# Building the last sixteen heads' convolution kernels during the first down stage instead of between two convolutions

## The chip, the cores and the metric

The kernel runs on one core of a Trainium2 chip. The metric is the device time of one execution in microseconds; the time of a version is the median over its runs.

## The reference

The input x has the shape (32, 64, 1024): 32 sequences in the batch, 64 heads, 1024 positions. Two stages follow one another, and x is added to the result.

```python
# stage 1: a state space convolution, one kernel of length 1024 per head
dtA = A * dt[:, None]                       # A = -exp(log_A_real) + i*A_imag, 64 states a head
K = 2.0 * einsum('hn,hnl->hl', C * (exp(dtA) - 1) / A, exp(dtA[:, :, None] * arange(1024))).real
u_m = u * mask                              # positions past a sequence's length are zero
y = causal_convolution(u_m, K) + u_m * D    # by FFT in the reference
y = y * mask
# stage 2: a gated feed-forward net over y as 2048 rows (32 x 64) of 1024, weights of 4 bits
inter = silu(y @ Wg) * (y @ Wu)             # Wg, Wu: 1024 x 2752, one scale and zero point per 128 rows
out = inter @ Wd                            # Wd: 2752 x 1024, likewise
x = x + out
```

## The kernel before, in words

**Blocks and stages.** The 2048 rows of stage 2 are cut into four blocks of 512, each of 16 heads times 32 sequences. Block 0 needs the convolutions of heads 0 to 15, block 1 those of 16 to 31, block 2 of 32 to 47 and block 3 of 48 to 63. The call `conv(blk)` makes a block's input; this text calls conv(2) the third convolution and conv(3) the fourth (by its index, the fourth is number 3). An input block lies in on-chip memory as two float16 tiles of 128 x 8 x 512, a rounded part and a remainder. There are two such pairs, `c.x[0]` and `c.x[1]`: blocks 0 and 2 use the first, 1 and 3 the second.

Matrix work is a list of chains that `roll` runs through (L773). Stage 0 and 1 are the first gate and up products of blocks 0 and 1, stage 2 (`pairs`) the rest of these for both blocks at once, stage 3 the down products of block 0, stage 4 those of block 1, stage 5 the gate and up products of blocks 2 and 3, stages 6 and 7 their down products. In stages 3 and 4 nothing reads `c.x[1]`, from the last gate and up product of stage 2 until the fourth convolution writes it.

**A chain.** A down chain (`dn_pair`, L718) takes 21 groups of 128 rows and half a group: for each it issues four matmuls (L732, L733), and then the sum in PSUM has to be multiplied by the ratio of two scales before the next group can be added. This rescale runs on VectorE (L637, one instruction over two banks) or on ScalarE (L640, two of one bank), whichever the planner expects to be done first (`rescale_two`, L635). Three chains are in work at a time in stages 3 and 4, so that TensorE has matmuls of two chains while the third is being rescaled. A down step below means the four matmuls of one group.

**A convolution head.** `conv_head` (L531) multiplies a Toeplitz matrix of the head's kernel with the head's input: 24 matmuls (L548) of 32 to 256 columns. The matrix tile, 128 x 2 x 1024 float16 or 512 KB, is read from `kpad` in DRAM by a load on the SP queue (`toeplitz`, L525), whose source rows overlap. Three buffers hold such tiles, and the load of a tile is placed three heads ahead, so it waits until the head three before it has been multiplied. Every two heads the product is masked (L560, VectorE), rounded (L563, ScalarE) and its remainder taken (L565, mostly POOL). Every four heads an input `u` is loaded (L503) and split (L507, L510).

**A convolution kernel.** It is made for 8 heads at a time: decays (`decays`: L175 on POOL, an Exp over 16 heads on ScalarE at L179), phases (`tables`: L192 to L204 on VectorE, Sin and Square at L207 and L209 on ScalarE), factors (L218 to L223, VectorE), then `make_kernel` (L421): one matmul for the skip term D (L425), eight small ones (L427), two copies out of PSUM (L430, L431) and two writes to `kpad` on the SP queue (L433).

**Who sets the order.** Side work is written as generators, listed by stage in `sides` (L1033). For each step of a chain `roll` adds a side's rate to its credit and takes a step of it for each whole credit. Sides whose third entry is None take a step only while the planner's clocks of VectorE and ScalarE are not far ahead of TensorE's (`room`, L327); the others take it in any case, and those marked True are finished before the stage is left. `c.forced` turns off the planner's pauses. The framework then orders each engine's instructions by priority and its own estimate of readiness.

In stages 3 and 4 the sides are the unpacking of the down weights, `fourth()` and `convs()`. `fourth()` (L996) makes the kernels of heads 48 to 63. It waits until all down weights are unpacked, closes the unpacking buffers and opens a pool `kg2` in their place; the decays lie in `c.x[1][0]`, the phases in `c.x[1][1]`, factors and kernels in `kg2`. `convs()` (L1017) runs the third convolution, then whatever is left of `fourth()` at one go with `c.forced` set, then the fourth. Its rate is 1.9 steps (eight make a head) for one step of a chain (`RATES`, L33).

Of the kernel before, what the change touches and what calls it, by code (L numbers as in the profile page):

```python
# [29 lines left out]
KSCALE = 64.0  # L30
PLACES = {("a", "pair"): 1, ("a", "single"): 2, ("b", "pair"): 3}
MAGIC = 12582912.0
RATES = {"first": (0.5, 4.6), "fill": (1.0, 0.8), "third": 0.5, "convs": 1.9}  # L33
HOP, MM, LANDING = 220.0, 215.7, 6000.0
LAG, HEAD_START, APART = 2, 2, 5
DVE_ROOM, ACT_ROOM = 1200.0, 1500.0
# [211 lines left out]
def every(gen):  # L248
    for _ in gen:
        pass  # L250
# [585 lines left out]
def tile_ssm_ffn(ctx, tc, io):  # L836
    nc = tc.nc
    c = Core(ctx, tc, io)
# [119 lines left out]
    def third():  # L958
        tiles = [c.cv.tile([128, 2, L], F16, name="t0", bufs=3) for _ in range(3)]
        small = [c.cv.tile([128, 8, 4, B], F16, name=k) for k in ("uh", "ul", "uh", "ul")]  # L960
        take = c.scratch(tiles[:2])
        c.prm = take([128, 5, H], F32)
        nc.sync.dma_start(c.prm, io["prm"])
        for _ in range(4):
            yield
        coefficients = head_coefficients(nc, nc.vector, co, take, c.prm, c.cst[:, 66:67], 32, 32)
        while True:
            with c.after("dve"), c.after("act"):
                if next(coefficients, "end") == "end":
                    break  # L970
            c.dve(1000)
            yield
        yield from c.decays(c.scratch(tiles[2:]), (32, 40))
        c.small = ScratchPool(c.scratch(small))
        c.taps(c.small, 32)
        for h0 in (32, 40):
            yield from c.tables(ScratchPool(c.scratch(tiles[:2])), h0, 8)
            yield from c.factors(c.small, h0, 8, c.xds[h0])

    third_it = third()  # L980
# [13 lines left out]
        return make  # L994

    def fourth():  # L996
        c.forced = True
        every(third_it)
        c.forced = False
        while not c.ready.issuperset(("dn", k, part) for k in range(4) for part in range(3)):  # L1000
            yield
        c.up_stack.close()
        with tc.tile_pool(name="kg2", bufs=1, side="right") as kg2:
            space = c.x[1]
            yield from c.decays(c.scratch(space[:1]), (48, 56))
            c.taps(kg2, 48)
            for h0 in (48, 56):
                yield from c.tables(ScratchPool(c.scratch(space[1:])), h0, 8)
                yield from c.factors(kg2, h0, 8, c.xds[h0])
                for _ in range(3):  # L1010
                    yield
                c.make_kernel(kg2, h0, 8, "a")
                yield

    fourth_it = fourth()

    def convs():  # L1017
        yield from c.conv(2)
        c.forced = True
        c.need(*(("dn", k, part) for k in range(4) for part in range(3)))  # L1020
        every(fourth_it)
        c.forced = False
        yield from c.conv(3)

    def residuals():
        take = c.scratch(c.x[0])
        c.res = [c.residual(take, n0, 3) for n0 in (0, 2, 4, 6)]
        c.last_o = c.scratch(c.x[1])
        yield

    convs_it = convs()
    second_it = second()
    sides = {  # L1033
        0: [(unpack_it, RATES["first"][0], None), (group_it, 1.0, None), (second_it, RATES["first"][1], True)],
        1: [(unpack_it, RATES["fill"][0], None), (third_it, RATES["fill"][1], None)],
        2: [(third_it, RATES["third"], None), (unpack_it, RATES["fill"][0], None)],
        3: [(unpack_it, RATES["fill"][0], None), (fourth_it, RATES["fill"][1], None), (convs_it, RATES["convs"], False)],
        4: [(fourth_it, RATES["fill"][1], None), (convs_it, RATES["convs"], True)],
        6: [(residuals(), 1.0, True)],
# [80 lines left out]
```

## Time and profile before

| | |
|---|---|
| median of 3 runs | 1079.41 us (1079.26 to 1080.23) |
| the profiled execution | 1076.19 us |
| its span, first to last instruction | 1074.4 us |
| TensorE busy | 1025.0 us, 95% |
| VectorE, ScalarE, POOL busy | 804.7, 773.7, 243.9 us |
| granted clock of TensorE | 0.997 |
| stages 3 and 4 with the third and fourth convolution | 400.1 us (first matmul of head 32) to 577.7 us (last of head 63) |
| heads 32 to 47, heads 48 to 63 | 400.1 to 485.4 us, 509.0 to 577.7 us |

The page gives busy times of one profiled execution by engine; the windows give the same for any stretch of it. PE stands for TensorE's matmuls, PEld for its weight loads, DVE for VectorE, ACT for ScalarE. A matmul is shown with its whole way through the array, so two neighbours overlap: a product of 512 columns is shown as 0.38 us, while the next one starts 0.216 us later. In a timeline the square brackets give an engine's idle time before an instruction, and after the arrow who ended it.

### The profile page before, as it was taken

The numbers are of one execution on the slowest core, as the hardware profiler recorded it, in microseconds if no ns is written. First come the engines' busy times: TensorE is split into PE (matmuls) and PEld (weight loads), VectorE is DVE, ScalarE is ACT, GpSimd is POOL, SyncE is SP. The second block draws the span as 40 slices with busy tenths as digits, with TensorE's granted clock in tenths as the row PEclk, the third lists the DMA queues.
The fourth block names the chain that finished last, engine by engine and source line by source line (L and its number), as shares of the span: only waits on it lengthen the run. The fifth ranks groups of instructions, "written<-read, shape, count | busy, mean of one in ns | idle before, by whom it ended". The sixth has DMA issues, their size and how long they took to land.

```text
span 1074.4 us, 15424 instructions
## 1 busy us (share of the span) xinstructions
PE 1025.0 (95%) x5854; PEld 512.6 (48%) x5854; DVE 804.7 (75%) x938; ACT 773.7 (72%) x1031; POOL 243.9 (23%) x272
## 2 busy tenths in 40 slices
PE   3989999999899999997999999999999999999996
PEld 3867444444344445663665444444444444444442
DVE  8964888888977786678456777777778777777775
ACT  5767778787677787778577777666666667778774
POOL 0334123232332333230112112222221111102002
PEclk9999999999999999999999999999999999999998
DMA  6976321111111424455752011000000002325002
GB/s 196 332 243 211 100 69 40 40 59 40 49 50 58 139 90 156 152 180 190 238 167 99 30 38 42 20 20 20 18 13 20 20 20 79 118 72 166 37 1 79
DMA packets 52099, 99.76 MB, mean 93 GB/s; under 512 B 9524, under 2 KB 11444, under 8 KB 52024
## 3 DMA queue, kind: packets, MB, share of 16 engines
q1 hardware_dynamic: 38888, 70.09, 20.1%
q0 software_dynamic: 5280, 17.31, 4.3%
q10 hardware_dynamic: 7856, 11.37, 3.6%
q8 instruction: 46, 0.75, 0.3%
q14 instruction: 29, 0.24, 0.1%
HBM read 78.99 MB, written 19.76 MB: 92 GB/s over the span
## 4 chain that ended last, share of the span: by engine, by line
PE 81%; DVE 7%; ACT 5%; DMA 3%; issue 2%; POOL 1%; DVEq 0%; SPq 0%; ACTq 0%; POOLq 0%
PE chq L687 23%; PE chq L688 22%; PE chq L732 12%; PE chq L733 12%; PE cq L548 6%; PE chq L664 2%; PE chq L665 2%; DMA t<-kpad 2%; ACT chq L640 1%; DVE chq L618 1%; DVE v L700 1%; ACT chq L620 1%; DMA ihl<-kpad 1%; ACT sg L695 1%; POOL spill L310 0%
## 5 line engine op out<-in xcount | busy, mean ns | idle before, releaser
L687 PE MATMUL chq<-xh,w 128*128 128x512 f16 x1216 | 459.4, 379 | 7.2 <-DVE chq L618 2.1
L688 PE MATMUL chq<-xl,w 128*128 128x512 f16 x1216 | 457.6, 379 | 0.0
L618 DVE TENSOR_SCALAR chq<-chq,gur 128x1024 f32<-128x1024 f32 x261 | 333.3, 1290 | 93.4 <-PE chq L688 91.8
L620 ACT ACTIVATE chq<-chq,gur 128x1024 f32<-128x1024 f32 x285 | 304.2, 1085 | 86.9 <-PE chq L688 84.4
L640 ACT ACTIVATE chq<-chq,dnr 128x512 f32<-128x512 f32 x358 | 232.8, 661 | 68.6 <-PE chq L733 62.8
L732 PE MATMUL chq<-ihl,wd 128*128 128x512 f16 x672 | 253.0, 379 | 8.9 <-ACT chq L640 5.2
L733 PE MATMUL chq<-ihl,wd 128*128 128x512 f16 x672 | 252.9, 379 | 0.0
L637 DVE TENSOR_TENSOR chq<-chq,dnr 128x1024 f32<-128x1024 f32 x141 | 173.1, 1230 | 81.0 <-PE chq L733 80.2
L688 PEld LDWEIGHTS <-w 128*128 128x128 fp8e4 x1216 | 118.6, 98 | 154.6 <-issue 18.5
L687 PEld LDWEIGHTS <-w 128*128 128x128 fp8e4 x1216 | 118.7, 98 | 146.7 <-issue 1.1
L310 POOL TENSOR_TENSOR ihl<-v,ihl 128x512 f16<-128x512 f32 x42 | 48.3, 1150 | 364.0 <-ACT ihl L629 364.0
L733 PEld LDWEIGHTS <-wd 128*128 128x128 fp8e4 x672 | 65.4, 97 | 81.0 <-issue 18.2
L548 PEld LDWEIGHTS <-t 128*128 128x128 f16 x1152 | 81.3, 98 | 38.7 <-DMA t<-kpad 5.8
L732 PEld LDWEIGHTS <-wd 128*128 128x128 fp8e4 x672 | 65.4, 98 | 67.2 <-issue 0.8
L548 PE MATMUL cq<-uh,t 128*128 128x256 f16 (+3 forms) x720 | 91.1, 226 | 4.1 <-DMA t<-kpad 4.0
L565 POOL TENSOR_TENSOR xl<-y,xh 128x512 f16<-128x512 f32 x28 | 36.4, 1301 | 161.0 <-ACT xh L563 161.0
L548 PE MATMUL cq<-ul,t 128*128 128x256 f16 (+3 forms) x360 | 71.6, 225 | 0.0
L629 ACT CAST ihl<-v 128x512 f16<-128x512 f32 x42 | 25.9, 617 | 58.7 <-DVE v L700 55.3
L700 DVE SCALAR_TENSOR_TENSOR v<-chq,gul,sg 128x1024 f32<-128x1024 f32 x38 | 48.6, 1280 | 17.2 <-PE chq L688 11.3
L310 POOL TENSOR_TENSOR spill<-v,spill 128x512 f16<-128x512 f32 x42 | 48.8, 1161 | 14.2 <-ACT spill L629 13.9
L640 ACT ACTIVATE chq<-chq,gur 128x512 f32<-128x512 f32 x66 | 43.2, 661 | 11.0 <-PE chq L665 9.8
L590 POOL TENSOR_TENSOR w<-w,z 128x256 int32<-128x256 int32 x42 | 31.6, 772 | 81.2 <-DVE w L584 76.9
(249 smaller groups left out, 812.5 us busy)
## 6 DMA issues: line engine op xcount, KB each, us to landing
t<-kpad SPq DMA_DIRECT2D x48, 512.0 KB, 4.3
spill<-spill POOLq DMA_DIRECT2D x42, 256.0 KB, 2.7
ihl<-spill ACTq DMA_DIRECT2D x42, 256.0 KB, 2.7
z<-zc SPq DMA_DIRECT2D x29, 256.0 KB, 3.7
u<-xF SPq DMA_DIRECT2D x12, 512.0 KB, 3.9
xr<-xT SPq DMA_DIRECT2D x12, 512.0 KB, 4.5
out<-xr POOLq DMA_DIRECT2D x24, 256.0 KB, 2.9
w<-qgu SPq DMA_DIRECT2D x21, 256.0 KB, 4.8
```

The lines of the kernel that those rows point to most:

```text
L310: self.nc.gpsimd.tensor_tensor(out, a, b, op)
L548: nc.tensor.matmul(q[:, d:, h % 2, :], t0[:, lw, 128 * d:128 * d + 128], uu[:, 0:8 - d, h % 4, :], start=(d == 0 and k == 0 and h % 2 == 0 ...
L565: split.tensor_tensor(xl[:, :, ts], yv, xh[:, :, ts], ALU.subtract)
L618: self.mark("dve", self.nc.vector.tensor_scalar(q, q, col, None, ALU.mult))
L620: self.mark("act", self.nc.scalar.activation(q, q, AF.Copy, scale=col))
L637: self.mark("dve", self.nc.vector.tensor_tensor(q, q, cols.to_broadcast([128, 2, 512]), ALU.mult))
L640: self.mark("act", self.nc.scalar.activation(q[:, k], q[:, k], AF.Copy, scale=cols[:, k]))
L687: nc.tensor.matmul(q[:, b], lw, xh[:, g, :], start=(g == 0), stop=False, skip_group_check=True)
L688: nc.tensor.matmul(q[:, b], lw, xl[:, g, :], start=False, stop=(g == GH - 1), skip_group_check=True)
L700: nc.vector.scalar_tensor_tensor(v, q, last, self.sg.pop(ct - 21), ALU.mult, ALU.mult)
L732: nc.tensor.matmul(q[:, j], lw, self.ihl[:, g, 0], start=(g == 0), stop=False, skip_group_check=True)
L733: nc.tensor.matmul(q[:, j], lw, self.ihl[:, g, 1], start=False, stop=False, skip_group_check=True)
```

## The change

`fourth()` no longer waits for the unpacked weights nor for the unpacking buffers: it starts with stage 3. All that it needs lies in the idle `c.x[1]`: decays in the first half of `c.x[1][0]`, the taps in a quarter of it, phases in seven eighths of `c.x[1][1]`, factors and kernels in what is left of both. The pause before `make_kernel` is now the planner's lead of VectorE over TensorE plus 220 ns, in place of three steps. `convs()` no longer runs `fourth()` at one go: after the third convolution it yields, step by step, until the kernel of heads 56 to 63 is known, and drives `fourth()` itself only when it is forced. The rate of `convs()` falls from 1.9 to 1.52 steps.

```diff
-RATES = {"first": (0.5, 4.6), "fill": (1.0, 0.8), "third": 0.5, "convs": 1.9}
+RATES = {"first": (0.5, 4.6), "fill": (1.0, 0.8), "third": 0.5, "convs": 1.52}
...
     def fourth():
-        c.forced = True
-        every(third_it)
-        c.forced = False
-        while not c.ready.issuperset(("dn", k, part) for k in range(4) for part in range(3)):
+        first, second = c.x[1]
+        yield from c.decays(c.scratch([first[:, :4]]), (48, 56))
+        c.taps(ScratchPool(c.scratch([first[:, 4:6]])), 48)
+        for h0 in (48, 56):
+            small = ScratchPool(c.scratch([first[:, 6:8], second[:, 7:8]]))
+            yield from c.tables(ScratchPool(c.scratch([second[:, :7]])), h0, 8)
+            yield from c.factors(small, h0, 8, c.xds[h0])
+            yield from c.pause(c.td - c.tp + HOP)
+            c.make_kernel(small, h0, 8, "a")
             yield
-        c.up_stack.close()
-        with tc.tile_pool(name="kg2", bufs=1, side="right") as kg2:
-            space = c.x[1]
-            yield from c.decays(c.scratch(space[:1]), (48, 56))
-            c.taps(kg2, 48)
-            for h0 in (48, 56):
-                yield from c.tables(ScratchPool(c.scratch(space[1:])), h0, 8)
-                yield from c.factors(kg2, h0, 8, c.xds[h0])
-                for _ in range(3):
-                    yield
-                c.make_kernel(kg2, h0, 8, "a")
-                yield
...
     def convs():
         yield from c.conv(2)
-        c.forced = True
-        c.need(*(("dn", k, part) for k in range(4) for part in range(3)))
-        every(fourth_it)
-        c.forced = False
+        while 56 not in c.known:
+            if c.forced:
+                next(fourth_it)
+            yield
         yield from c.conv(3)
```

## The prediction

> **What bounds the kernel now.** I read the page first, then the busy time by window, then the TensorE timeline where the windows showed a hole, then the loads of the Toeplitz tiles.
>
> The page names TensorE:
>
> ```profile
> span 1074.4 us, 15424 instructions
> PE 1025.0 (95%) x5854; PEld 512.6 (48%) x5854; DVE 804.7 (75%) x938; ACT 773.7 (72%) x1031; POOL 243.9 (23%) x272
> ```
>
> The change leaves the number of matmuls as it is, so it can gain only where PE waits. The windows (PE, PEld, DVE, ACT, POOL busy, then clock and DMA) say where:
>
> ```profile
> 425.00:475.00 50.00, 50.00 (x398) 30.46 (x397) 34.06 (x41) 36.46 (x56) 13.67 (x18) 1.00 0.47 151
> 475.00:485.00 10.00, 9.69 (x82) 5.93 (x80) 8.14 (x9) 6.67 (x11) 5.35 (x7) 1.00 0.79 261
> 485.00:517.00 32.00, 24.11 (x198) 13.49 (x197) 23.00 (x39) 22.56 (x37) 1.77 (x3) 1.00 0.65 209
> 517.00:567.00 50.00, 50.00 (x399) 30.41 (x397) 26.31 (x25) 36.32 (x56) 8.03 (x8) 1.00 0.58 183
> ```
>
> PE is never idle from 425 to 475 and from 517 to 567, and idles 7.9 us from 485 to 517. That is where `convs()` runs the whole of `fourth()` at once, between the third and the fourth convolution. The timeline shows its six long waits (start, duration, then the idle time and who ended it):
>
> ```profile
> 491.62 0.38 PE L732 MATMUL chq<-ihl,wd 128*128 128x512 f16 x1 [1.45 <-ACT chq L640]
> ...
> 494.98 0.38 PE L732 MATMUL chq<-ihl,wd 128*128 128x512 f16 x1 [1.48 <-DVE chq L637]
> ...
> 498.27 0.38 PE L732 MATMUL chq<-ihl,wd 128*128 128x512 f16 x1 [1.14 <-ACT chq L640]
> ...
> 502.89 0.38 PE L732 MATMUL chq<-ihl,wd 128*128 128x512 f16 x1 [1.85 <-ACT chq L640]
> ...
> 508.98 0.28 PE L548 MATMUL cq<-uh,t 128*128 128x256 f16 x1 [0.87 <-DMA t<-kpad]
> ...
> 511.67 0.28 PE L548 MATMUL cq<-uh,t 128*128 128x256 f16 x1 [1.00 <-DMA t<-kpad]
> ```
>
> Four times a down chain waits for its rescale, which stands behind table work on VectorE or ScalarE; twice the convolution waits for its first Toeplitz tiles. Every number rests on the load of such a tile (L525, 512 KB), issue to landing, from 425 to 475 and from 505 to 520:
>
> ```profile
> DMA to landing us min/median/max: 3.4/3.6/4.6
> ...
> DMA to landing us min/median/max: 3.7/4.9/6.0
> ```
>
> **What goes.** The six waits sum to 7.79 us. A matmul is shown as 0.38 us but the next starts 0.216 later, so each wait hides 0.16 more: 8.8. Two shorter holes (starts 0.27 and 0.15 later than that pitch, at 495.62 and 499.65) make 9.2 us. The kernel matmuls L425 and L427 stay and cost the same.
>
> **What is moved, and stays as much.** From the groups between 405 and 585: VectorE's table, factor and copy work for 16 heads (L192 to L204 9.1 us, L218 to L223 4.0, L431 0.8) is 13.9 us; ScalarE's (two table loads 2.6, L179 1.1, L207 2.0, L209 2.0, L430 0.7) is 8.4. POOL's two L175 stand where they stood in the built order. In it the work now lies among the rescales of the first down stage and of the early second one: the kernel of heads 48 to 55 comes half way through head 43, that of 56 to 63 at the end of head 47. There VectorE is 68% and ScalarE 73% busy (34.06 and 36.46 of 50). The fourth group's steps are taken only while the planner has room, so rescales go to the other engine. Low bound: nothing, as 425 to 475, where unpacking of weights is taken in the same way, loses nothing. High bound: 9.2 us, what the same 22.3 us of work costs in its present place. The nearest dense stretch is 395 to 405, where VectorE is busy 9.18 and ScalarE 9.66 of 10 us and PE idles 0.59. I take 1.5 us, that rate over some 25 us of the added work.
>
> For the table loads row and rule differ. The rows, of ScalarE's timeline:
>
> ```profile
> 484.07 1.36 ACT L640 ACTIVATE chq<-chq,dnr 128x512 f32<-128x512 f32 x2 [1.08 <-PE chq L733]
> 485.45 1.28 ACT L179 ACT_TABLE_LOAD   x1
> 486.74 1.06 ACT L179 ACTIVATE xh<-xh 128x1024 f32<-128x1024 f32 x1
> ```
>
> The load begins 0.02 us after the rescale before it, and its Exp begins as it ends. The Trainium skill (ScalarE: Activation LUTs, What ACT_TABLE_LOAD costs) adds a drain of some 1380 ns to each switch, which would speak against putting two switches among rescales: an estimate from it is 2.8 us more on ScalarE, and a forecast of -1.1 instead of -3.9 if all of it fell on the path. The trace shows no such drain, so it is not in the sum.
>
> **Queues passed.** On SP the tap load L440 now waits, ahead of two residual loads and a tile load, for the last gate/up read of x[1]; head 35's tile behind it waits for head 32 anyhow: nothing. The four kpad writes (L433) stand ahead of tile loads 46 and 51, two residual loads (L768, which wait for output DMAs to land) ahead of 46 and 47: tile 46 is issued by my count some 5 us before its head, against a load of 3.6; nothing, and one for one if it is over 1.4 us later. The first output of heads 48 and 49 must wait until x[1]'s scratch has been read; it stands 13 down steps of 0.86 us (four matmuls) after the last kernel: covered. No later Sin or Silu load is added: the built order has ten table loads in both.
>
> **What is added: a burst.** `convs` runs at 1.52 steps instead of 1.9 for each step of a chain, also while it waits for head 56. The built order shows the result. Before, the 64th head ends together with the 133rd down step, matmuls of both mixed to the end. After, at that step only head 55 and two matmuls of head 56 are done; the second down stage ends its share, the convolution must be finished (it is marked True), and 190 convolution matmuls follow without a down matmul between them, heads 56 to 63. Nothing else is left for PE in that time.
>
> One head takes 1.54 us (511.67 to the next matmul at 513.21). There are three tile buffers: the tile of head h+3 can be issued only when head h has ended. With a load L, 0.1 us to trigger and wake (an estimate; the issue at 510.70 follows head 48's last matmul, which ends at 510.68) and 1.54 us of matmuls, three heads take L + 1.64 instead of 4.62. Counted from the burst's start: head 55 ended at -1.08, so tile 58 is issued then; 56 ends at 1.40, 57 at 2.95. With L = 4.9, the median where loads followed one another: 58 starts 3.95 (1.0 late) and ends 5.5; 59 starts 6.4 (0.9 late), ends 7.95; 60 is in time, ends 9.5; 61 starts 10.5 (1.0), ends 12.05; 62 starts 12.95 (0.9), ends 14.5; 63 ends 16.05. Lost: 3.8 us. With L = 3.4, the shortest, 0.8 us; with 6.0, the longest here, 6.0 us. I take 3.8: in the burst's first half the outputs of two chains (four of 256 KB) move too, as in the stretch that gave 4.9. The Trainium skill (DMA: Bandwidth & Descriptors, Anatomy of one DMA) has a rule of 2.0 us plus bytes over 436 GB/s; for 512 KB that is an estimate of 3.2 us, a loss of 0.4 and a sum of -7.3. The rows are above it wherever loads follow one another, so they decide.
>
> After the burst both orders are alike (first gate/up of x[0], eight down matmuls between), so the 0.77 us wait at 580.01 stays.
>
> **The sum.** -9.2 + 1.5 + 3.8 = -3.9 us. The profiled run took 1076.19 us, 3.2 under the median of the runs, 1079.41; so 1072.3 for a profiled run and 1075.5 for the median.
>
> **Rivals.** *The burst is nearly free* (tiles land in 3.4 us, table work is hidden): -9.2 + 0.8 = -8.4, 1071.0. For it: the lone loads from 425 to 475. Against: 4.9 at 505 to 520.
>
> *The burst eats the gain*: L = 6.0 with outputs and a residual load beside it, 6.0, and 1 to 4 us of rescales: -2.2 to +0.8, 1077.2 to 1080.2. For it: 5.96 for one load at 505.67, and 3.7 MB of tiles in some 16 us beside 1 MB of outputs, with 209 GB/s over 485 to 517. Against: loads there come in pairs after a pause, those of the burst one by one.
>
> *Slower: the table work costs its rescales as much wherever it stands.* In the hole 22.3 us of it cost 9.2, 0.41 us for each. If three chains without slack pay the same in the first down stage, nothing is gained and the burst is added: +3.8, 1083.2. It is slower by 0.2% from 7.6 us on, 0.34 for each us. For it: rescales are in order behind the tables, and convolution matmuls that fill their waiting are thinner (1.52). Against: it is no longer forced, and 425 to 475 has 15.9 us of free VectorE.
>
> That the change does not do what it says is answered by the order: the kernel of heads 48 to 55 now stands inside the third convolution, and the fourth follows with no stretch of table work before it.
>
> **How the numbers follow.** A measurement of this kernel tells 0.2%, 2.2 us, from no change. Forecast (-2.2 to -7, so 1072.4 to 1077.2) 0.47; nearly free 0.15; eaten 0.18; slower 0.20. Faster: 0.62, same 0.18, slower 0.20. The range starts at the cheap burst, 1071.0, and ends at 1082.5, which leaves out about half of the slower case.
>
> **What would show it.** Right: no PE wait over 1 us between 485 and 550 (my count puts the burst at 556 to 573); then a stretch of some 16 us with L548 alone on PE, four waits of about 1 us for t<-kpad, convolution over near 573.8; VectorE and ScalarE near idle in it. Wrong: waits for L637 or L640 spread over 410 to 500 that sum to more than 5 us; tile loads over 6 us in the burst; or a tile load held behind an L433 or L768 on SP.

## The result and the profile after

The changed kernel takes 1081.02 us (median of 20 runs, 1078.49 to 1082.19) against 1078.69 us for the kernel before (20 runs, 1076.26 to 1083.9). The ratio is 1.0020, with a 95% interval of 1.0011 to 1.0028: slower by 2.2 us (1.2 to 3.0), where 3.9 us less had been forecast. The profiled execution took 1081.07 us. The page of the kernel after begins:

```profile
span 1079.3 us, 15440 instructions
...
PE 1028.1 (95%) x5854; PEld 513.3 (48%) x5854; DVE 813.0 (75%) x942; ACT 767.6 (71%) x1023; POOL 245.4 (23%) x272
```

The span is 4.9 us longer than before, with the same 5854 matmuls. Not all of this is the change: the execution profiled before took 1076.19 us, 2.5 less than its median, the one after lies at its median. TensorE was held up for longer, or ran at a lower clock, in some stretch. The windows of the kernel after (busy time of PE, PEld, DVE, ACT and POOL, then clock, DMA share, GB/s) say where:

```profile
425.00:475.00 50.00, 48.52 (x356) 27.91 (x355) 39.94 (x53) 37.25 (x60) 13.47 (x17) 1.00 0.41 130
475.00:485.00 10.00, 10.00 (x82) 5.74 (x81) 7.99 (x13) 8.49 (x15) 4.00 (x5) 1.00 0.76 231
485.00:517.00 32.00, 29.94 (x204) 16.27 (x203) 23.78 (x28) 19.10 (x32) 3.68 (x5) 0.95 0.74 234
517.00:567.00 50.00, 49.79 (x387) 29.96 (x386) 28.24 (x28) 38.41 (x60) 9.01 (x10) 1.00 0.58 182
567.00:585.00 18.00, 12.53 (x169) 10.72 (x168) 5.79 (x7) 3.49 (x6) 5.82 (x7) 1.00 0.59 198
```

From 485 to 517 PE idles 2.1 us in place of 7.9, so the hole has gone. But 425 to 475, which lost nothing before, now loses 1.5 us, and the clock in 485 to 517 is 0.95. The last line is new: 18 us with the convolution almost alone on PE, which idles 5.5 us of them, while VectorE and ScalarE are busy 5.8 and 3.5 us. That is the forecast burst. Its waits, from PE's timeline:

```profile
567.88 0.28 PE L548 MATMUL cq<-uh,t 128*128 128x256 f16 x1 [0.16 <-DMA t<-kpad]
572.67 0.28 PE L548 MATMUL cq<-uh,t 128*128 128x256 f16 x1 [3.10 <-DMA t<-kpad]
575.24 0.28 PE L548 MATMUL cq<-uh,t 128*128 128x256 f16 x1 [0.87 <-DMA t<-kpad]
579.04 0.28 PE L548 MATMUL cq<-uh,t 128*128 128x256 f16 x1 [0.58 <-DMA t<-kpad]
581.49 0.28 PE L548 MATMUL cq<-uh,t 128*128 128x256 f16 x1 [0.76 <-DMA t<-kpad]
```

One wait of 3.1 us stands among three of 0.6 to 0.9, near the forecast size of about 1 us. Its tile, of head 59, was issued at 566.23 and was there at 572.67: 6.4 us. By the completion signals in the trace the six loads of the burst (heads 58 to 63) took 4.2, 6.4, 7.4, 6.9, 4.6 and 4.5 us. The second to fourth of them were on the way together, and the wait for the second hid most of the lateness of the next two. Four outputs of 256 KB were issued from 564.6 to 568.8, beside those three loads, and took 4.0 to 6.3 us; the same four outputs took 2.3 to 2.8 us in the kernel before, where they started at 576.4 to 579.5 with no tile load beside them.

What else PE waited for from 400 to 600 (line that waited, who ended it, us in total, times, longest):

```profile
PE cq L548 <- DMA t<-kpad: 5.5, 5, 3.1
PE chq L732 <- DVE o L751: 2.3, 2, 2.0
PE chq L732 <- DVE wd L599: 0.8, 1, 0.8
PE chq L732 <- ACT chq L640: 0.6, 2, 0.3
```

Waits for rescales have almost gone (0.6 us). In their place stands one of 2.0 us for L751, the scaling of a finished down chain on VectorE, which frees the bank for the next chain. VectorE, POOL and PE around it:

```profile
484.03 1.38 DVE L201 SCALAR_TENSOR_TENSOR xl<-xl 128x256 f32<-128x256 f32 x1
485.33 1.64 DVE L203 SCALAR_TENSOR_TENSOR xl<-xl,cst 128x512 f32<-128x512 f32 x1
...
487.29 0.74 DVE L751 TENSOR_SCALAR o<-chq,dnl 128x512 f16<-128x512 f32 x1
```

```profile
483.60 1.53 POOL L565 TENSOR_TENSOR xl<-y,xh 128x512 f16<-128x512 f32 x1 [0.98 <-ACT xh L563]
485.09 1.33 POOL L760 TENSOR_TENSOR xr<-xr,o 128x512 f32<-128x512 f32 x1
```

```profile
488.08 0.38 PE L732 MATMUL chq<-ihl,wd 128*128 128x512 f16 x1 [2.04 <-DVE o L751]
...
491.07 0.63 PE L733 MATMUL chq<-ihl,wd 128*128 128x512 f16 x1
491.50 0.63 PE L732 MATMUL chq<-ihl,wd 128*128 128x512 f16 x1
```

L751 stands behind the second group's phases. Two of these took 1.38 and 1.64 us while POOL worked; in the hole before, with POOL idle, they took 0.41 and 0.74 us. The difference, 1.9 us, is about the whole wait. Soon after it, from 488.94 until 492.35, PE ran at half its clock: a down matmul is shown as 0.63 us and the next starts 0.43 later, in place of 0.38 and 0.216.

For the experiments TensorE's time lost is counted as well: for each pair of matmuls, the distance of their starts less the usual one for that number of columns, summed from 395 to 590. It comes to 14.0 us before and 17.8 after, in one execution each.

| stretch, us | before | after |
|---|---|---|
| 440 to 485 | 0.8 | 3.5 |
| 485 to 515 | 9.9 | 4.6 |
| 560 to 590 | 1.4 | 7.2 |

### The profile page after: what moved, and what is told of

It is laid out like the page before. It is cut to its first block, busy times and chain, and to the rows that moved or that the text cites. A ratio compares the mean times of both kernels' runs of the same rounds, so it can differ in the third digit from the quotient of the medians.

```text
span 1079.3 us, 15440 instructions
## 1 busy us (share of the span) xinstructions
PE 1028.1 (95%) x5854; PEld 513.3 (48%) x5854; DVE 813.0 (75%) x942; ACT 767.6 (71%) x1023; POOL 245.4 (23%) x272
## 4 chain that ended last, share of the span: by engine, by line
PE 77%; DVE 8%; ACT 6%; issue 5%; DMA 3%; POOL 1%; SPq 0%; DVEq 0%; POOLq 0%; ACTq 0%
PE chq L687 21%; PE chq L688 21%; PE chq L732 12%; PE chq L733 12%; PE cq L548 5%; PE chq L665 2%; PE chq L664 2%; ACT chq L640 2%; DMA t<-kpad 2%; DVE chq L618 1%; DVE v L700 1%; ACT chq L620 1%; DMA ihl<-xF 1%; POOL spill L310 1%; ACT sg L695 1%
## 5 line engine op out<-in xcount | busy, mean ns | idle before, releaser
L640 ACT ACTIVATE chq<-chq,dnr 128x512 f32<-128x512 f32 x350 | 227.5, 661 | 75.2 <-PE chq L733 68.5
L637 DVE TENSOR_TENSOR chq<-chq,dnr 128x1024 f32<-128x1024 f32 x145 | 177.1, 1230 | 75.5 <-PE chq L733 75.0
L565 POOL TENSOR_TENSOR xl<-y,xh 128x512 f16<-128x512 f32 x28 | 36.8, 1313 | 126.6 <-ACT xh L563 126.6
```

What stands on the lines that cost most here:

```text
L565: split.tensor_tensor(xl[:, :, ts], yv, xh[:, :, ts], ALU.subtract)
L637: self.mark("dve", self.nc.vector.tensor_tensor(q, q, cols.to_broadcast([128, 2, 512]), ALU.mult))
L640: self.mark("act", self.nc.scalar.activation(q[:, k], q[:, k], AF.Copy, scale=cols[:, k]))
```

## The experiments

A ratio is always to the kernel before, from runs on the same chip; one thousandth is 1.08 us. The question is which of three things gave the hole's gain back: the table work among the rescales, the late tile loads of the burst, or the new pace of the convolutions.

### The changed kernel without its tables, without its late loads, without both

The first run drops the decays, phases and factors of heads 48 to 63 and keeps the planner's bookings and the order; the second gives heads 58 to 63 an older tile in place of a load; the third does both.

```diff
-        yield from c.decays(c.scratch([first[:, :4]]), (48, 56))
+        for _ in range(4):
+            yield
+        c.act(4000)
...
-            yield from c.tables(ScratchPool(c.scratch([second[:, :7]])), h0, 8)
-            yield from c.factors(small, h0, 8, c.xds[h0])
+            c.fac[h0] = [plain.tile([128, 8, 32], F32, name=k) for k in ("e1t", "e2t")]
+            for e in c.fac[h0]:
+                nc.gpsimd.memset(e, 0.0)
...
```

```diff
-                self.t0[k] = self.toeplitz(k)
+                self.t0[k] = self.toeplitz(k) if k < 58 else self.t0[k - 3]
```

> The changed kernel without the table work of heads 48 to 63: their decays, phases and factors are left out (the factors are set to zero by POOL), so their convolution kernels hold the skip term alone and the output is not the reference's. The planner's bookings and pauses stay, so matmuls and the burst of eight heads stand as in the changed kernel. Theory A (the changed kernel pays twice: about 6.3 us in the burst, about 7 us to table work among the rescales between 440 and 495 us): that second loss goes, 2.3 - 6.5, about 4 us faster than before. Theory B (the burst is the cost, and the losses from 440 to 495 come from the thinner convolution, the change of stages and the loads queued there, with or without tables): within 1.5 us of the changed kernel, about 2 us slower than before.

> The changed kernel without the loads of the Toeplitz tiles of heads 58 to 63: each takes the tile of the head three before it, so the output is not the reference's. The matmuls stand in the same order. Theory A (in the burst PE waits for these loads): the waits of 3.1, 0.9, 0.6 and 0.8 us go, about 5.5 to 6 us faster than the changed kernel, 3 to 4 faster than before. Rival (the burst waits for the masking of its products, or for the split of its input, which the loads only hide): under 2 us faster than the changed kernel.

> Both left out: table work of heads 48 to 63 and tile loads of heads 58 to 63. If theory A's two losses are separate they add: about 2.3 - 6.5 - 6 = 10 us faster than before. If one feeds the other (the table work delays outputs and loads, which then crowd the burst), less than the sum: 6 to 8 us faster.

Measured: without tables 1076.49 us, 0.9992 (0.9984 to 1.0001); without late loads 1073.74 us, 0.9964 (0.9951 to 0.9976); without both 1071.04 us, 0.9941 (0.9929 to 0.9952). Against 1.0020 the tables cost 3.0 us, the loads 6.0, both together 8.5, each good to some 1.5 us: close to the sum of the two. The tables cost about twice the 1.5 us of the prediction's sum, and about half as much as the loads: the run without them lies between what the two theories expected of it. The run without loads did what its theory A said (3.9 us faster than before). The run without both is 6.4 us faster than before, not 10; this is not because one loss feeds the other, but because the tables cost 3.0 and not 6.5. In the run without tables the waits for tiles remain (from PE's waits, 400 to 600) and the one for L751 is not there:

```profile
PE cq L548 <- DMA t<-kpad: 4.0, 3, 3.2
PE chq L732 <- DVE wd L599: 0.8, 1, 0.8
```

So the larger cost is that of the loads. And 440 to 485 still loses 2.6 us without tables: something else is in that stretch, and is taken up below.

### Steps paid back: no burst

`convs` waits for the kernel of head 56 and takes its credit without work meanwhile. Here the steps spent waiting are given back two for one, at the old pace.

```diff
-RATES = {"first": (0.5, 4.6), "fill": (1.0, 0.8), "third": 0.5, "convs": 1.52}
+RATES = {"first": (0.5, 4.6), "fill": (1.0, 0.8), "third": 0.5, "convs": 1.9}
...
+        owed = 0
         while 56 not in c.known:
...
+            owed += 1
             yield
-        yield from c.conv(3)
+        for n, _ in enumerate(c.conv(3)):
+            if n % 2 and owed:
+                owed -= 1
+            else:
+                yield
```

> The changed kernel at the old pace of 1.9, and the steps that the third convolution's end spends waiting for heads 56 to 63 are paid back afterwards, two convolution steps for one. The built order has no burst: the 64th head ends with the 133rd down step, as in the kernel before. Table work stays among the rescales, and for 18 down steps after head 48 hardly any convolution is mixed in. Theory A: the burst's 6 us go, about 3 to 4 us faster than before. Rival (the stretch without convolution costs what the burst did, since three chains alone leave no slack for tables): 0 to 4 us slower than before.

Measured: 1070.04 us, 0.9929 (0.9916 to 0.9941): 7.6 us less than before and 9.8 less than the changed kernel. The time lost on PE falls to 6.5 us, with 1.3 in 440 to 485 and 1.9 in 485 to 515. The tables are all there and stand where the change put them.

### The pace alone, and the place of the tables alone

```diff
-RATES = {"first": (0.5, 4.6), "fill": (1.0, 0.8), "third": 0.5, "convs": 1.9}
+RATES = {"first": (0.5, 4.6), "fill": (1.0, 0.8), "third": 0.5, "convs": 1.52}
```

This edit to the kernel before is the first run, its reverse in the changed kernel the second.

> The kernel before with one edit, the pace of the convolutions 1.52 in place of 1.9; the tables of heads 48 to 63 stay between the two convolutions, so the hole stays. In the built order the last seven heads then follow the first down stage without a down matmul between them. Theory (the burst's loads and the thinner pace are a cost of their own, whatever is done with the tables): the hole's 9.2 us stay, the burst adds 5 to 6 us and the thinner convolution 1 to 2, so 6 to 8 us slower than before, ratio 1.0055 to 1.0075. Rival (the pace costs little by itself; it is the table work among the rescales that pushes the convolution back): ratio 0.999 to 1.002.

> The changed kernel with the pace of before, 1.9: the tables begin with the first down stage, nothing else. In the built order the fourth convolution still waits for the kernel of heads 56 to 63, and its last six heads follow the first down stage in a row. Theory (the burst costs by its length, the thin pace costs 1 to 2 us beside it): loads lose some 4 us in place of 6.0, the thinner pace nothing, so 3 to 4 us less than the changed kernel: ratio to before 0.998 to 0.999. Rival one (the pace is the whole loss): no slower than the kernel that pays its steps back, 0.993. Rival two (where the tables stand is the loss): 1.002 as the changed kernel.

Measured:

| | pace 1.9 | pace 1.52 |
|---|---|---|
| tables between the convolutions | 1 (before) | 1.0066 (1.0052 to 1.0080) |
| tables with the first down stage | 0.9975 (0.9965 to 0.9984) | 1.0020 (1.0011 to 1.0028) |

The new place of the tables gains 2.7 us at the old pace and 5.0 at the new one; the new pace costs 7.1 us with the tables in their old place and 4.9 with them in the new one. So the whole loss comes from one number in the line `RATES`: at the old pace the change would have been a gain. The windows of the run with the pace alone show its two parts, and the hole still there in the middle:

```profile
425.00:485.00 60.00, 58.97 (x450) 34.74 (x448) 40.89 (x49) 43.42 (x66) 17.78 (x22) 1.00 0.49 153
485.00:517.00 32.00, 28.40 (x169) 13.74 (x168) 25.45 (x39) 22.39 (x37) 2.25 (x3) 0.95 0.53 162
...
556.00:590.00 34.00, 29.97 (x280) 20.93 (x279) 14.13 (x16) 19.20 (x31) 10.80 (x13) 0.95 0.50 172
```

PE's lost time rises by 1.5 us in 440 to 485 (0.8 to 2.3), with no table work there, and by 5.3 in 560 to 590. At the old pace with the tables moved, six heads still follow the down stage, and the waits for tiles are 4.2 us: so rival one of that run, which had the pace as the whole loss, falls, and rival two, which had the place, falls with it. What the two leave is the burst, made by the pace and by the wait for the kernel together.

### A fourth buffer, and smaller outputs: why are the tiles late?

```diff
-            t0 = self.cv.tile([128, 2, L], F16, name="t0", bufs=3)
+            t0 = self.cv.tile([128, 2, L], F16, name="t0", bufs=4)
...
-        for k in range(hh, hh + (16 if hh < 16 else 6 if hh < 32 else 3)):
+        for k in range(hh, hh + (16 if hh < 16 else 6 if hh < 32 else 4)):
...
```

```diff
+        w = 16 if blk == 1 else 512
...
-            (nc.gpsimd if blk < 3 else nc.scalar if 2 * k + j == 7 else nc.sync).dma_start(self.io["out"][128 * n:128 * n + 128, 512 * blk:512 * blk + 512], xr[:, j])
+            (nc.gpsimd if blk < 3 else nc.scalar if 2 * k + j == 7 else nc.sync).dma_start(self.io["out"][128 * n:128 * n + 128, 512 * blk:512 * blk + w], xr[:, j, :w])
```

> The changed kernel with a fourth buffer for Toeplitz tiles from head 32 on, the load of a tile placed four heads ahead. Theory one (each load beside outputs takes some 6.4 us however many are on the way): four heads take 6.4 + 1.6 us in place of 4 x 1.54 = 6.2, so a burst of eight heads loses some 2 to 3 us in place of 6.0: 3 to 4 us less than the changed kernel, ratio to before 0.998 to 0.999. Theory two (the loads and the outputs share a bandwidth, one more load on the way makes each longer): the loss stays 5 to 6 us, ratio 1.001 to 1.002.

> The changed kernel, of whose block 1 only 16 of 512 columns are written to the output: eight outputs of 256 KB, four of them in the burst, become 8 KB each. The loads of the Toeplitz tiles and everything else stay. Theory (the loads are late because they share the DMA engines with the outputs): tile loads in the burst land in 3.6 to 4.6 us, the burst loses 1 to 3 us in place of 6.0, so 3 to 5 us less than the changed kernel, ratio to before 0.9975 to 0.999. Rival (they are late by themselves, three buffers being too few for a head in 1.54 us): loads stay near 5 us and more, ratio 1.001 to 1.002.

Measured: four buffers 1077.08 us, 0.9996 (0.9987 to 1.0005), 2.6 us less than the changed kernel; small outputs 1075.37 us, 0.9979 (0.9970 to 0.9988), 4.4 less. With four buffers, PE's waits, the landing of the tiles issued from 556 to 575, and the window after the last wait:

```profile
PE cq L548 <- DMA t<-kpad: 4.1, 2, 2.3
```

```profile
DMA to landing us min/median/max: 4.9/6.6/8.2
```

```profile
575.00:580.00 5.00, 5.00 (x54) 4.58 (x52) 0.69 (x1) 0.62 (x1) 1.15 (x1) 0.66 0.04 17
```

The line on landing counts only the two loads, of six, whose completion is paired with their issue. The completion signals give all six: 4.9, 4.1, 6.3, 8.7, 8.5 and 8.2 us. The last four were on the way together beside the same four outputs, where in the changed kernel three loads took 6.4 to 7.4. So more loads on the way made each later, as theory two has it; the time of the run lies between the two theories. Part of what the waits gave back (5.5 to 4.1 us) went again to a clock of 0.66 behind them. With small outputs the waits are short, as are the loads (those issued from 556 to 575, four of seven counted):

```profile
PE cq L548 <- DMA t<-kpad: 2.6, 4, 1.0
```

```profile
DMA to landing us min/median/max: 3.3/4.4/5.7
```

The long wait of 3.1 us is gone; four of at most 1.0 us stay. The three loads that had taken 6.4, 7.4 and 6.9 us took 3.4, 4.3 and 4.1. In the profiles the burst loses 3.1 us less (4.1 against 7.2); from 485 to 515 another 1.6 us less is lost, as the half clock at 489 did not occur there. So about half of the loads' 6.0 us came from the outputs beside them. The rest stands beside loads of 3.3 to 4.6 us; with three buffers a load has two heads, 3.1 us, before TensorE waits for it. That this is the reason for the rest was not tested by itself: the fourth buffer made the loads longer.

### Three more ways to spread the fourth convolution

```diff
-        3: [(unpack_it, RATES["fill"][0], None), (fourth_it, RATES["fill"][1], None), (convs_it, RATES["convs"], False)],
+        3: [(fourth_it, RATES["fill"][1], None), (unpack_it, RATES["fill"][0], None), (convs_it, RATES["convs"], False)],
```

The first run adds this line to the kernel that pays its steps back; the second is the changed kernel with only `"convs": 2.4`; the third is the first with 2.1.

> The kernel that pays the waiting steps back (pace 1.9), with the steps of the tables taken before those of the unpacking at each chain step. In the built order the kernel of heads 56 to 63 then stands some ten down steps earlier and the fourth convolution is spread more evenly; there is no burst. Theory (what is left to gain is the waiting of the convolution for that kernel): 0 to 2 us less than without this edit, ratio to before 0.991 to 0.993. Rival (the unpacked weights come later, and the down chains wait for them): 1 to 4 us more than without it, ratio 0.994 to 0.997.

> The changed kernel with one number edited, the pace of the convolutions 2.4 in place of 1.52; no step is paid back. In the built order the third convolution ends ten down steps earlier, the fourth waits for its kernels, and head 63 ends with the 133rd down step: no burst. Theory (the length of the burst decides, however it is avoided): as the kernel that pays its steps back, ratio to before 0.992 to 0.995. Rival (a pace over 1.9 takes the convolution's rounding and masking too close to the rescales of the first down stage): 0.996 to 1.000.

> The kernel that pays its steps back and takes the table steps first, at a pace of 2.1 in place of 1.9: in the built order head 63 ends at down step 123 and ten down steps follow without a convolution matmul between them. Theory (a convolution that ends early leaves the last down steps without matmuls to fill the wait for their rescales): 0 to 3 us more than at 1.9, ratio to before 0.992 to 0.996. Rival (its loads and tables, spread earlier, still gain): 1 us less, 0.991 to 0.992.

Measured: tables first 1069.57 us, 0.9925 (0.9913 to 0.9937); pace 2.4 alone 1068.87 us, 0.9919 (0.9907 to 0.9932); tables first at 2.1 1076.70 us, 0.9988 (0.9979 to 0.9997). The order of the sides makes no difference that can be told. The single number 2.4 gives a version that is 8.7 us faster than before, as good as any other here. Its PE waits from 400 to 600 no longer contain a tile:

```profile
PE chq L732 <- DVE chq L637: 0.8, 1, 0.8
PE chq L732 <- ACT chq L640: 0.5, 2, 0.3
PE chq L732 <- DMA ihl<-spill: 0.5, 1, 0.5
```

The last run was worse than its theory's end of 0.996. Its loss is not where that theory looked: 6.7 us are lost from 455 to 485, with 2.1 us of waits for unpacked weights (L599), 1.3 for a factor (L223) and 1.3 for L751, and only 2.2 in the last down steps. The waits suggest that the convolution there ran ahead into work that VectorE had not done yet; which part of it (pace, order or paying back) is decisive was not tried.

## Why the prediction was wrong

**The hole: right.** All six long waits are gone and no table stretch is left between the convolutions. The runs without burst show what that is worth with whatever the moved table work costs there: 7.6 to 8.7 us. The same two terms of the sum give 9.2 - 1.5 = 7.7.

**The table work, taken at 1.5 us: too small in this order.** It measured 3.0. The working spread it as a rate over a dense stretch and looked at rescales alone, which can go to the other engine. It came as one wait of 2.04 us for another instruction, L751, behind two of VectorE's phases stretched from 1.2 to 3.0 us beside POOL, and in the profile a stretch at half clock behind that. "No PE wait over 1 us between 485 and 550" failed by this one. The drain at a table load, which was kept out of the sum, was rightly kept out: the two table loads that moved, at 418.10 and 441.38, start 0.02 us after the instruction before them, the next instruction starts 0.01 after their end, and waits for ScalarE's rescales are 0.6 us in all. The rival of equal cost everywhere, 9.2 us, is three times what was measured.

**The burst, taken at 3.8 us: too small, and decisive.** Its length (heads 56 to 63, 565 to 583), its idle VectorE and ScalarE and its late tiles came as described. The loads cost 6.0 us, the upper end of the working, which had been put to loads of 6.0 us each; the six took 5.7 in the mean, from 4.2 to 7.4. The first step that failed is "I take 3.8", and in it the reason given for loads of 4.9 us: that outputs move in the burst "as in the stretch that gave 4.9". No output was on the way in that stretch. The last ones before it had landed at 488.68, the next were issued at 565.08; all that the kernel before issued from 505 to 525 is this:

```profile
t<-kpad SPq DMA_DIRECT2D x8, 512.0 KB, 4.9
ihl<-spill ACTq DMA_DIRECT2D x4, 256.0 KB, 2.8
kpad<-kb SPq DMA_DIRECT2D x2, 16.0 KB, 4.6
```

So 4.9 us is a load's time without outputs, and beside four outputs it was 6.4 to 7.4. The kernel before already has a case: a tile load issued at 565.17 beside two outputs took 5.2 us, and the outputs 5.0 and 5.1. For an estimate the prediction had also named the Trainium skill (DMA: Bandwidth & Descriptors, Anatomy of one DMA), 3.2 us for 512 KB. The section gives its fit for transfers issued from GpSimd; these are issued from SP. Loads of 3.3 to 8.7 us in these runs stand above it, by most where several transfers are on the way. Nothing on SP held a tile back in the burst: the residual load that waited for outputs was issued at 558.37, before it.

**The pace as such: missing from the sum.** A convolution step at 1.52 gives TensorE less to do between the down steps of three chains. That was named in a rival and priced nowhere. The pace alone adds 1.5 us of lost time in 440 to 485.

With the measured terms, -9.2 + 3.0 + 6.0 + 1.5 = +1.3, at the low end of the interval of 1.2 to 3.0. About 1 us stays unexplained: the run without tables and late loads gained 6.4 us, where -9.2 + 1.5 gives 7.7. The forecast time of 1075.5 was missed by 5.5 us; the rival "the burst eats the gain" (-2.2 to +0.8, loads near 6 us and 1 to 4 us of rescales) describes what happened, with an end 1.4 us too low. A better reading was there: the prediction read in the order that the slower pace makes the burst, and could have asked what that number costs with the tables in their old place. It costs 7.1 us, more than the whole gain that was forecast.

## What to carry to other kernels

Price each number of a change by itself: the new place of the tables gained 2.7 to 5.0 us and the new pace took 4.9 to 7.1, and only the two together were on offer. When side work is paced by credit and has to wait for something, credit that lapses returns as a burst at the end; look in the built order for what is left without partners, and give it its transfers' time with everything else that is issued there. Take a load's duration from a stretch with the same company: here it was 3.4 to 4.6 us in a quiet stretch, 4.9 beside other loads and 6.4 to 7.4 beside four outputs.

## What was not expected of the hardware

**VectorE beside POOL.** L201 and L203 read two tensors from on-chip memory. Their groups in the kernel before, with POOL idle (in 485 to 517 it is busy 1.77 us, none of them beside these instructions), were:

```profile
L201 DVE SCALAR_TENSOR_TENSOR xl<-xl x2: 414/414/415, 491.1 to 499.6; 128x256 f32<-128x256 f32 x2
L203 DVE SCALAR_TENSOR_TENSOR xl<-xl,cst x2: 742/742/742, 491.4 to 498.9; 128x512 f32<-128x512 f32 x2
```

After, one of them takes 1.38 us and ends 0.28 after POOL's L565; L203 takes 1.64 and ends 0.55 after POOL's L760. The Trainium skill (SBUF — State Buffer, SBUF: two separate sides) has it that such an instruction and a POOL instruction that reads this memory shut one another out for a whole instruction. The ends agree with that. The other runs shift these instructions against POOL's, so they test the dependence. Of the 22 L201 in all versions that have them, 13 overlap no POOL instruction and took 0.41 to 0.42 us. Nine overlap one: eight took 0.95 to 1.66 and ended 0.28 or 0.29 after POOL's, and the ninth, which began 0.21 before POOL's, took 0.42. So the stretching goes with POOL; why it does is the page's account, not shown here.

**Half the clock after a short wait.** After the wait of 2.04 us at 488 PE ran at half clock from 488.94 to 492.35, that is 3.41 us, and lost some 1.3 us more than the wait. With four buffers the same came after waits of 1.80 and 2.28 us, from about 575.3 to 578.7. It came also in the run with the pace alone, after waits of 2.39 us (clock 0.66 from 487 to 492) and 3.61 us (0.61 from 576 to 580), and in the run without tables with a wait of 3.19 us (0.59 from 567 to 571). It did not come after the wait of 3.10 us at 572.67, nor after the same wait of 2.04 us in the run without late loads. The Trainium skill (TensorE: Matmul & The Clock Gate, Part 1: The HAM clock gate) tells of a free-running window of some 3.4 us; the length of the slow stretch agrees, but waits shorter than the window sufficed here. It shows in the scatter of one kernel: of the 20 runs of the kernel before beside the last experiments, the four with a mean clock of 0.992 or 0.993 took 1078.7 to 1080.0 us, the four with 0.997 took 1076.2 to 1078.0. What decides in which execution it comes stays open.
